# Perceiver layer on one core: ScalarE copies the last pair's transposed weights, and unit 6's projection of values moves behind the last output projection

## The chip, the core and the metric

The kernel runs on one core of one Trainium2 chip. The core has TensorE (PE, matrix products), VectorE (DVE), ScalarE (ACT), GpSimd (POOL) and SyncE (SP, which here issues most transfers). The metric is device time in microseconds (us), lower is better. Times of before and after are medians of several runs. The trace is one execution taken by the hardware profiler.

## What is computed

One layer of a perceiver, in float32, on `x` of 64 sequences x 32 tokens x 256 features, with a context of 257 rows of 192 features for each sequence. The reference, cut down:

```python
x = x + cross_attention(layernorm(x), ctx, mask, Wq, Wk, Wv, Wo)     # 16 heads of 16
x = x + local_attention(layernorm(x), Wq, bq, Wk, bk, Wv, bv)        # one head, each token sees 2 on each side
h = layernorm(x).reshape(2048, 256)
e = argmax(h @ Wr + br)                                              # one of 8 experts for each token
x = x + (gelu(gelu(h @ W1[e] + b1[e]) @ W2[e] + b2[e]) @ W3[e] + b3[e])
```

## The kernel before, in words

The work has three stages. PE, DVE, ACT and POOL each run their instructions in the order in which the program writes them down (`manual_schedule`, L190), so every order below is one written by hand; SP's queue keeps program order too. An engine that waits holds up all that stands behind it on that engine.

**The loop over pairs** (L941 to L987) does the cross attention of two sequences at a time, 32 pairs, as a pipeline: in step m the scores of pair m (`scores_mm`, `numerators`) are made while pair n = m-1 has its softmax weights turned (`transposed`, L783) and pair n-1 is multiplied with its values (`attend`, L799), reduced to its own heads (`own`, L818) and, every second pair, projected and added to `xs` (`project_out`, L834). `transposed` turns four 128x512 pieces through PE (L791) into PSUM and copies each to the tile `pt` in SBUF, by DVE (L797), or for one piece of some steps by ACT (L795). `attend` reads `pt`. GpSimd scales the weights `p` ahead of the turn (L778). Two more steps than pairs are needed: in step m = 32 the last pair (31) is turned, in step m = 33 it is attended, owned and projected out.

**The local attention** goes by units of 256 tokens, 8 of them, and is woven into the loop by `between` (L879). For a unit: normalise (`normed_in`), turn to `xnT` (`turn_in`), `project_q` into `tT`, `project_v` (L371: four products on PE, two ACT copies to `av`, three small GpSimd steps on its extra columns), `attend_scores` (L399), `attend_least` (DVE), `attend_exps` (ACT), `attend_weights`, `attend_sums`, `attend_3` (DVE), `normed_out` (L475, which writes the unit's rows to the DRAM table `table_x` by a transfer on SP's queue). `route_2` to `route_4` find the expert of each token and put it into a table of slots. Unit 6 is the last that starts in the loop: its `project_v` is in step m = 32 (L891) and its `attend_scores` in step m = 33 behind the last `own` (L958). Its remaining steps and the whole of unit 7 stand behind the loop (L1066 to L1098), since unit 7 needs the last `project_out`. PSUM has eight banks, which `bank` hands out (L193).

**The experts** (from L1361) go by tiles of 128 slots, with weights in a ring of three sets (L991). `fetch` (L1001) loads one set with four transfers on SP's queue: `wa` 1030 KB, `bo` 128 KB, `wb` 2048 KB, `wc` 512 KB. `fetch(2, 0)` and `fetch(1, 1)` (L1018) stand right behind the loop; their memory is that of the loop's pools, so the first of them waits until the loop's last users are done. Then come, on the same queue, the two `table_x` writes of units 7 and 6 (L479), then a third fetch (L1363), which waits for the small tile `go` (L1127), made from the finished table of slots. GpSimd gathers an expert tile's rows from `table_x` (`gather_rows`, L1030) when the writes have landed, and PE turns them (`turn`, L1149). Between the loop and that turn PE also works on an "early" tile whose rows were gathered before the loop ended: `early_first` (L1045), `early_second` (L1061), and then `second` (L1289).

Of the kernel before, what the change touches and what calls it, by code (L numbers as in the profile page):

```python
# [7 lines left out]
F32 = mybir.dt.float32  # L8
I32 = mybir.dt.int32
U8 = mybir.dt.uint8  # L10
AF = mybir.ActivationFunctionType
# [7 lines left out]
P = 128  # L19
# [21 lines left out]
NV = D + 2 * E + 1  # L41
# [74 lines left out]
def perceiver_layer_kernel(  # L116
# [14 lines left out]
    nc = tc.nc  # L131
# [237 lines left out]
        proj[u] = [tT]  # L369

    def project_v(u, norm, col):  # L371
        xt = xnT[u]
        v = lw.tile([P, 2, NV], F32, name="av")
        for i in range(2):
            ps = bank("av", (NV,))
            for k in range(2):
                nc.tensor.matmul(
                    ps, xt[:, k, i * P : (i + 1) * P], lv[:, k, :], start=k == 0, stop=k == 1
                )
            nc.scalar.copy(v[:, i, :], ps)  # L380
        part = v[:, :, D : D + E]
        nc.gpsimd.tensor_tensor(
            part, part, bvw.unsqueeze(1).to_broadcast([P, 2, E]), ALU.add
        )
        part = v[:, :, D + E : D + 2 * E]
        nc.gpsimd.tensor_tensor(
            part, part, norm.std[:, col : col + 2].unsqueeze(2).to_broadcast([P, 2, E]), ALU.mult
        )
        nc.gpsimd.tensor_scalar(
            v[:, :, NV - 1], v[:, :, NV - 1], sim_one, None, ALU.add  # L390
        )
        proj[u].append(v)

    def attend_1(u):
        attend_scores(u)
        attend_least(u)
        attend_exps(u)

    def attend_scores(u):  # L399
        tT, v = proj[u]  # L400
        xt = xnT.pop(u)
        ps = bank("as", (2, P))
        for i in range(2):
            cols = slice(i * P, (i + 1) * P)
            for k in range(2):
                nc.tensor.matmul(
                    ps[:, i, :], tT[:, k, cols], xt[:, k, cols], start=k == 0, stop=k == 1
                )
        soft[u] = ps

    def attend_least(u):
        ps = soft[u]
        _, v = proj[u]
        nmx = sp.tile([P, 2], F32, name="anmx")
        p = lw.tile([P, 2, P], F32, name="ap")
        for i in range(2):
            nc.vector.scalar_tensor_tensor(
                p[:, i, :], ps[:, i, :], v[:, i, NV - 1 : NV], k_["band"], ALU.add, ALU.add
            )
        nc.vector.tensor_reduce(nmx, p, AX.X, ALU.min)  # L420
        soft[u] = (p, nmx)
# [171 lines left out]
    NP = B // 2  # L593
    with tc.tile_pool(name="xq", bufs=1) as qpool, tc.tile_pool(
# [185 lines left out]
                    )  # L780
            prob[n] = p

        def transposed(n, parts, by_act=False):  # L783

            if n not in pT:
                pT[n] = wp.tile([P, 2, 2, 512], F32, name="pt")
            for k in parts:
                j, t = divmod(k, 2)
                ps = bank("t")
                for i in range(4):  # L790
                    nc.tensor.transpose(  # L791
                        ps[:, i * P : (i + 1) * P], prob[n][:, j, i, t * P : (t + 1) * P], ident
                    )
                if by_act and k == 3:
                    nc.scalar.copy(pT[n][:, j, t, :], ps)  # L795
                else:
                    nc.vector.tensor_copy(pT[n][:, j, t, :], ps)  # L797
# [81 lines left out]
        def between(m, entered, weights):  # L879


            k, r = divmod(m, 4)
            if r == 0:
                if k >= 1:
                    norms[k] = Norm()
                if k <= 5:
                    norms[k].moments(0, xs[:, 2 * (k + 2), :])
                if 1 <= k <= NU:
                    norms[k].moments(2, xs[:, 2 * (k - 1), :])
                if 0 <= k - 2 <= NU - 2:  # L890
                    project_v(k - 2, norms[k - 1], 2)  # L891
                    if k - 2 < NU - 2:
                        attend_1(k - 2)
                    else:

                        nc.scalar.activation(sp.tile([P, 1], F32, name="spare"), eps_col, AF.Sqrt)
            if r == 1:
                if k <= 5:
                    norms[k].moments(1, xs[:, 2 * (k + 2) + 1, :])
                if 1 <= k <= NU:  # L900
                    norms[k].moments(3, xs[:, 2 * (k - 1) + 1, :])
                if 1 <= k + 1 <= NU - 1:
                    queries_in(k + 1, norms[k - 1], 0, xn=entered)
                if weights:
                    attend_3(k - 2, norms[k], 4, attend_sums(weights))
                if k <= 7:
                    norms[k].newton(slice(0 if k <= 5 else 2, 2 if k == 0 else 4 if k == 1 else 6))
                if 0 <= k - 3 <= NU - 3:
                    enter_table(route_4(2 * (k - 3), 2))
                if k == EARLY + 2:  # L910
                    nc.vector.tensor_copy(token0, table[:, 0:1])
                    early_gather()
            if r == 2:
                if 0 <= k - 1 <= NU - 2:
                    turn_in(k - 1, entered)
                if 1 <= k + 1 <= NU - 1:
                    queries(k + 1)
                if 0 <= k - 2 <= NU - 3:
                    route_2([k - 2], [norms[k].rstd[:, 4:6]])
            if r == 3:  # L920
                if k == EARLY + 1:
                    ps = bank("gap", (1,))
                    nc.tensor.matmul(
                        ps, k_["ones"], before[:, 2 * EARLY, 0:1], start=True, stop=True
                    )
                    gap = sp.tile([P, 1], F32, name="gap")
                    nc.vector.tensor_scalar(gap, ps, -1.0 / P, 1.0, ALU.mult, ALU.add)
                    nc.vector.scalar_tensor_tensor(
                        before[:, 2 * EARLY, 0:1], gap, 0.0, before[:, 2 * EARLY, 0:1],
                        ALU.max, ALU.add,  # L930
                    )
                if k == 0:
                    fold_scores()
                if k == 0:
                    fold_router()
                if 0 <= k - 1 <= NU - 2:
                    project_q(k - 1)
                if 0 <= k - 2 <= NU - 3:
                    route_3(2 * (k - 2), 2)

        for n in range(-1, NP + 1):  # L941
            m = n + 1
            k, r = divmod(m, 4)
            entered = weights = None
            if m < NP:
                if m % 2 == 0 and m // 2 + 2 < B // BG:
                    load(m // 2 + 2)
                if m % 2 == 1 and m // 2 + 1 < B // BG:
                    masks(m // 2 + 1)
                if m + 2 < NP:  # L950
                    centre(m + 2)
                scores_mm(m)
                numerators(m, range(0, 4))
            if 0 <= n - 1:
                attend(n - 1)
                own(n - 1)
            if n - 1 == NP - 1:
                attend_scores(NU - 2)  # L958
            if m < NP:
                numerators(m, (4,))  # L960
            if m + 1 < NP:
                keys_mm(m + 1)
            if r == 1 and 1 <= k + 1 <= NU - 1:
                entered = normed_in(k + 1, norms[k - 1], 0)
            if r == 2 and 0 <= k - 1 <= NU - 2:
                entered = normed_in(k - 1, norms[k], 2)
            if m < NP:
                numerators(m, range(5, 8))
                tail = last_1(m)
            if m + 1 < NP:  # L970
                values_mm(m + 1)
            if r == 3 and 0 <= k - 2 <= NU - 3:
                normed_out(k - 2, norms[k], 4)
            if 0 <= n < NP:
                transposed(n, (0,))
            if m < NP:
                last_2(m, tail)
            if r == 1 and 0 <= k - 2 <= NU - 3:
                weights = attend_weights(k - 2)
            if 0 <= n < NP:  # L980

                transposed(n, (1, 2, 3), r in (1, 2) and 4 < m < NP)
            if n - 1 == NP - 1:
                early_turn()
            if 0 <= n - 1:
                project_out(n - 1)
            between(m, entered, weights)  # L987


# [75 lines left out]

    u, v = NU - 2, NU - 1  # L1066
    norm = norms[NU]
    norm.root(slice(2, 4))
    xn = normed_in(v, norm, 2, True)
    attend_least(u)  # L1070
    turn_in(v, xn, True)
    attend_exps(u)
    project_q(v)
    project_v(v, norm, 2)
    attend_scores(v)
    weights = attend_weights(u)
# [404 lines left out]
```

## Time and profile before

| what | value |
|---|---|
| median of 3 runs | 673.88 us (671.67 to 674.72) |
| the profiled execution: its time | 671.86 us |
| the profiled execution: its span, first to last instruction | 670.1 us |
| mean granted TensorE clock in it | 0.988 of full |
| PE busy | 643.2 us, 96% of the span |
| ACT, POOL, DVE busy | 341.8, 345.0, 320.3 us |
| transfers | 85.51 MB |

The last `own` ends 400.21 us into the span, the rows of the first regular expert tile are turned from 433.57 us on, and the last instruction stands at 670.1 us. A row of the timeline gives the start, the length, the engine, the line, the operation with what it writes and reads, and in brackets how long the engine stood idle before it and for whom. A row of the windows gives for a stretch of time the busy time of each engine, the clock that was granted to TensorE, the share of the 16 DMA engines' time that packets took, and GB/s. A row of the waits gives who waited for whom, in total, how often, and the longest.

### The profile page before, as it was taken

How to read it: one execution, taken by the hardware profiler on the slowest of the kernel's cores; microseconds unless marked ns; L12 is line 12 of the kernel's file. 1: busy time of each engine (PE TensorE's matmuls, PEld its weight loads, DVE VectorE, ACT ScalarE, POOL GpSimd, SP SyncE). 2: the span in 40 equal slices, each digit the busy share in tenths (PEclk: the TensorE clock that was granted, in tenths of full speed). 3: DMA queues.
4: the chain of work that ended last, by engine and by line, in shares of the span. 5: the costliest groups of instructions: out<-in, count | busy, mean ns of one | idle time of the engine just before them, and what ended most of it. 6: DMA issues, size and time to landing. Idle time of an engine off the chain costs nothing. (4 is left out here: it accounts for less than half of the span.)

```text
span 670.1 us, 18642 instructions
## 1 busy us (share of the span) xinstructions
PE 643.2 (96%) x7033; PEld 532.3 (79%) x7033; DVE 320.3 (48%) x1211; ACT 341.8 (51%) x1054; POOL 345.0 (51%) x724
## 2 busy tenths in 40 slices
PE   6999999999999999999999997899999999999994
PEld 4777777677777777877877876899989898899894
DVE  3595676776876877777786785600000000000000
ACT  2864785585684775775766644433322222243220
POOL 2694585688588588588587561331313222231120
PEclk9998999999999999999999998899999999999998
DMA  8923213203313312222200019765793628961001
GB/s 320 295 98 103 76 35 100 104 10 128 105 25 114 104 53 89 101 73 72 97 34 1 19 37 351 253 222 177 245 344 96 217 86 255 336 221 40 27 17 27
DMA packets 37350, 85.51 MB, mean 128 GB/s; under 512 B 2513, under 2 KB 7890, under 8 KB 37024
## 3 DMA queue, kind: packets, MB, share of 16 engines
q1 hardware_dynamic: 34240, 74.64, 33.1%
q0 software_dynamic: 2912, 8.65, 4.0%
q8 instruction: 72, 1.18, 0.7%
q14 instruction: 126, 1.03, 0.5%
HBM read 103.64 MB, written 6.56 MB: 164 GB/s over the span
## 5 line engine op out<-in xcount | busy, mean ns | idle before, releaser
L752 ACT ACTIVATE p<-p,nmx 128x256 f32<-128x256 f32 x256 | 127.2, 500 | 69.0 <-DVE nmx L747 68.0
L778 POOL TENSOR_SCALAR p<-p,rd 128x256 f32<-128x256 f32 x256 | 117.8, 482 | 81.5 <-DVE rd L775 31.4
L1289 PE MATMUL moe<-h,wb 128*128 128x128 f32 (+3 forms) x992 | 128.9, 288 | 0.3 <-issue 0.3
L1289 PEld LDWEIGHTS moe<-h,wb 128*128 128x128 f32 x992 | 124.1, 191 | 2.1 <-issue 0.5
L1313 DVE TENSOR_TENSOR y<-moe,xb 128x256 f32<-128x256 f32 (+2 forms) x20 | 8.5, 423 | 218.5 <-PE moe L1309 208.0
L747 DVE CUSTOM_DVE_ANT_0 p<-s,mb 128x256 f32<-128x256 f32 x256 | 108.0, 478 | 4.6 <-PE s L725 4.6
L797 DVE COPY pt<-t 128x512 f32<-128x512 f32 x114 | 72.6, 674 | 49.8 <-PE t L791 49.8
L692 PE MATMUL k<-cp,pack 64*128 64x512 f32 x384 | 93.8, 609 | 0.0
L709 PEld LDWEIGHTS v<-pack,cp 64*128 64x128 f32 x768 | 78.2, 187 | 19.4 <-issue 8.5
L678 POOL TENSOR_SCALAR cp<-ct,pack 128x256 f32<-128x256 f32 x189 | 88.4, 485 | 8.6 <-DMA ct<-in_ctxt 6.8
L709 PE MATMUL v<-pack,cp 64*128 64x256 f32 x768 | 90.6, 376 | 0.0
L1314 POOL DMA_INDIRECT out_x<-y,token x20 | 20.2, 1009 | 131.3 <-DVE y L1313 110.9
L1279 ACT ACTIVATE h<-moe,wa 128x128 f32<-128x128 f32 (+3 forms) x120 | 38.6, 380 | 69.2 <-PE moe L1273 62.4
L1300 ACT ACTIVATE h<-moe,wa 128x128 f32<-128x128 f32 (+3 forms) x64 | 23.2, 381 | 96.4 <-PE moe L1289 90.7
L1273 PEld LDWEIGHTS moe<-xT,wa 128*128 128x128 f32 x480 | 60.4, 191 | 8.7 <-issue 5.1
L1273 PE MATMUL moe<-xT,wa 128*128 128x128 f32 (+3 forms) x480 | 64.2, 291 | 3.1 <-ACT h L1279 2.4
L791 PE MATMUL t<-pack,p 128*128 128x128 f32 x512 | 64.6, 277 | 0.2
L791 PEld LDWEIGHTS t<-pack,p 128*128 128x128 f32 x512 | 55.6, 141 | 11.0 <-issue 5.0
L692 PEld LDWEIGHTS k<-cp,pack 64*128 64x128 f32 x384 | 38.7, 188 | 32.0 <-issue 25.5
L752 ACT ACTIVATION_READ_ACCUMULATOR p<-p,nmx 128x1 f32 x256 | 48.5, 190 | 0.0
L1030 POOL DMA_INDIRECT xt<-table_x,token x24 | 25.1, 1046 | 43.7 <-issue 18.9
L810 PEld LDWEIGHTS pv<-pt,v 128*32 128x32 f32 x2048 | 30.9, 111 | 13.5 <-issue 5.0
(200 smaller groups left out, 833.9 us busy)
## 6 DMA issues: line engine op xcount, KB each, us to landing
wb<-in_WB SPq DMA_DIRECT2D x17, 2048.0 KB
ct<-in_ctxt SPq DMA_DIRECT2D x15, 1542.0 KB
wa<-in_WA SPq DMA_DIRECT2D x17, 1030.0 KB
wc<-in_WC SPq DMA_DIRECT2D x17, 512.0 KB
table_x<-aw SPq DMA_DIRECT2D x8, 512.0 KB
bo<-in_b SPq DMA_DIRECT2D x17, 128.0 KB
m<-in_mask SPq DMA_DIRECT2D x16, 128.5 KB
xs<-in_x SPq DMA_DIRECT2D x1, 1536.0 KB
```

The lines of the kernel that those rows point to most:

```text
L678: engine.tensor_scalar(cp[:, r, j, :], loaded[b // BG][0][:, r, b % BG, 0:KL], -1.0, clast[:, r, b : b + 1], ALU.mult, ALU.add,)
L692: nc.tensor.matmul(ps[c], wk[h, r, :], cp[h, r, :, :].rearrange("p b k -> p (b k)"), start=r == 0, stop=r == 2,)
L709: nc.tensor.matmul(ps[t][:, j * D : (j + 1) * D], cp[h, r, j, t * P : (t + 1) * P], wv[h, r, :], start=r == 0, stop=r == 2,)
L747: nc.vector.tensor_tensor_reduce(out=p[:, j, i, :], in0=ps[i][:, j * KL : (j + 1) * KL], in1=mb[:, b % BG, 0:KL], scale=1.0, scalar=mb[:, ...
L752: nc.scalar.activation(p[:, j, i, :], p[:, j, i, :], AF.Exp, bias=nmx[:, j, i : i + 1], scale=-1.0, accum_out=sums[:, j, i : i + 1],)
L778: nc.gpsimd.tensor_scalar(p[:, j, i, :], p[:, j, i, :], rd[:, j, i : i + 1], 1.0, ALU.mult, ALU.mult)
L791: nc.tensor.transpose(ps[:, i * P : (i + 1) * P], prob[n][:, j, i, t * P : (t + 1) * P], ident)
L797: nc.vector.tensor_copy(pT[n][:, j, t, :], ps)
L810: nc.tensor.matmul(pv[32 * i : 32 * i + 32, c, j, :], v[:, t, j, at : at + 32], pt[:, j, t, i * P + 64 * c : i * P + 64 * c + 64], start=t ...
L1273: nc.tensor.matmul(ps[:, i, 0:n], wa[:, at : at + P], x_j[:, c, 0:n], start=c == 0, stop=c == 1,)
L1279: nc.scalar.activation(h1[:, f + i, 0:n], ps[:, i, 0:n], AF.Gelu, bias=wa[:, at : at + 1])
L1289: nc.tensor.matmul(pss[f], wb[:, c, f * P : (f + 1) * P], h1[:, c, 0:n], start=c == 0, stop=c == F1 // P - 1,)
```

## The change

It has three parts, all within the last two steps of the loop and the first lines behind it.

1. In step m = 32 the four pieces of pair 31's turned weights are copied by ACT instead of DVE.
2. Unit 6's `project_v` leaves step m = 32. Its four products go behind the loop, that is behind the last `project_out` and `route_4`'s two products on PE. Its ACT copies and GpSimd steps go behind `turn_in` of unit 7. Its `attend_scores` moves forward to where `project_v` was, ahead of pair 31's `attend`. `project_v` is split into a PE part and the rest; for the other units the order of instructions stays the same.
3. Behind the loop, `attend_least` and `attend_exps` of unit 6 go behind unit 7's `project_q`; one activation on a spare tile ahead of `project_q` makes ACT load the table for exponentials there.

```diff
     def project_v(u, norm, col):
+        project_v_out(u, norm, col, project_v_mm(u))
+
+    def project_v_mm(u):
         xt = xnT[u]
-        v = lw.tile([P, 2, NV], F32, name="av")
-        for i in range(2):
-            ps = bank("av", (NV,))
+        pss = [bank("av", (NV,)) for _ in range(2)]
+        for i, ps in enumerate(pss):
             for k in range(2):
                 nc.tensor.matmul(
                     ps, xt[:, k, i * P : (i + 1) * P], lv[:, k, :], start=k == 0, stop=k == 1
                 )
+        return pss
+
+    def project_v_out(u, norm, col, pss):
+        v = lw.tile([P, 2, NV], F32, name="av")
+        for i, ps in enumerate(pss):
             nc.scalar.copy(v[:, i, :], ps)
...
-                if by_act and k == 3:
+                if k in by_act:
                     nc.scalar.copy(pT[n][:, j, t, :], ps)
...
                 if 0 <= k - 2 <= NU - 2:
-                    project_v(k - 2, norms[k - 1], 2)
                     if k - 2 < NU - 2:
+                        project_v(k - 2, norms[k - 1], 2)
                         attend_1(k - 2)
                     else:
+                        attend_scores(k - 2)
 
                         nc.scalar.activation(sp.tile([P, 1], F32, name="spare"), eps_col, AF.Sqrt)
...
-            if n - 1 == NP - 1:
-                attend_scores(NU - 2)
...
-                transposed(n, (0,))
+                transposed(n, (0,), (0,) if m == NP else ())
...
-                transposed(n, (1, 2, 3), r in (1, 2) and 4 < m < NP)
+
+                transposed(
+                    n, (1, 2, 3),
+                    (1, 2, 3) if m == NP else (3,) if r in (1, 2) and 4 < m < NP else (),
+                )
...
     u, v = NU - 2, NU - 1
     norm = norms[NU]
+    values = project_v_mm(u)
     norm.root(slice(2, 4))
     xn = normed_in(v, norm, 2, True)
+    turn_in(v, xn, True)
+    project_v_out(u, norms[NU - 1], 2, values)
+
+    nc.scalar.activation(sp.tile([P, 1], F32, name="spare"), eps_col, AF.Exp)
+    project_q(v)
     attend_least(u)
-    turn_in(v, xn, True)
     attend_exps(u)
-    project_q(v)
     project_v(v, norm, 2)
     attend_scores(v)
     weights = attend_weights(u)
```

More of the change, by code (lines that the diff above doesn't have):

```diff
@@ L399, in attend_scores @@
     def attend_scores(u):
-        tT, v = proj[u]
-        xt = xnT.pop(u)
+        tT = proj[u][0]
+        xt = xnT[u]
         ps = bank("as", (2, P))
@@ L413, in attend_least @@
         _, v = proj[u]
+        del xnT[u]
         nmx = sp.tile([P, 2], F32, name="anmx")
@@ L781, in last_2, with transposed @@
             prob[n] = p
-        def transposed(n, parts, by_act=False):
+        def transposed(n, parts, by_act=()):
             if n not in pT:
```

## Prediction

> **What bounds the kernel now.** I read the page first: PE is busy 96% of the span, so at most places only PE's own work counts, and the question is where PE waits. All edits lie between 394 and 425 us. I then followed the chain of waits back from the end: from 433.57 on it is PE, one piece behind another. Ahead of that it is this (start, length, what):
>
> ```profile
> 420.60 0.34 DVE aw L252
> ...
> 421.47 6.34 DMA table_x<-aw
> ...
> 428.61 4.92 DMA xt<-table_x,token
> 433.57 0.44 PE moe L1149 x2
> ```
>
> So PE's turn at 433.57 waits for a gather, the gather for two writes to `table_x`, and these seem to wait for DVE's end of the local attention. But the write takes 6.34 us. One such write in the loop (L479 at 392.44) is through the DMA engines by about 394.8, that is in 2.4. Why is this one longer? I looked at the windows, 2 us each:
>
> ```profile
> core 0: us, PE busy (x) PEld busy (x) DVE busy (x) ACT busy (x) POOL busy (x), PEclk, DMA share, GB/s
> 400.00:402.00 2.00, 2.00 (x16) 1.90 (x16) 0.57 (x2) 0.71 (x3) 0.00 (x0) 1.00 0.17 27
> 402.00:404.00 2.00, 0.42 (x4) 0.23 (x3) 1.66 (x7) 0.42 (x2) 0.00 (x0) 1.00 0.92 306
> 406.00:408.00 2.00, 2.00 (x6) 1.55 (x6) 0.19 (x1) 1.97 (x5) 0.00 (x0) 0.50 0.92 298
> 416.00:418.00 2.00, 2.00 (x19) 1.97 (x18) 1.89 (x6) 0.21 (x1) 0.00 (x0) 1.00 1.05 382
> 424.00:426.00 2.00, 2.00 (x13) 2.00 (x12) 0.98 (x5) 0.19 (x1) 0.67 (x1) 0.58 0.88 339
> 426.00:428.00 2.00, 2.00 (x21) 2.00 (x20) 0.66 (x4) 0.00 (x0) 0.00 (x0) 1.00 0.06 23
> ```
>
> From 402 to nearly 426 all 16 DMA engines are full, with the two weight fetches (7.4 MB). The `table_x` writes stand behind them on SP's queue. They land at 427.81, when the last engine has drained (0.06 of 16 engines is one). Even if DVE had been done 4 us sooner, they would have landed no sooner. What started the stream? SP's waits and its timeline:
>
> ```profile
> SPq L1008 <- DVE own L824: 7.3, 1, 7.3
> ```
>
> ```profile
> 400.28 0.56 SPq L1008 DMA_DIRECT2D wa<-in_WA  x1
> ...
> 420.99 0.90 SPq L479 DMA_DIRECT2D table_x<-aw  x2
> 428.91 0.61 SPq L1008 DMA_DIRECT2D wa<-in_WA  x1
> ```
>
> The first transfer of the stream waits for `own` of the last pair (399.87 to 400.21). So the chain that counts is: last `own`, 25.5 us of full DMA engines to 427.81, gather, PE. The local attention of units 6 and 7 beside it has some 4.4 us to spare (421.4 against 425.8). Last I read PE's timeline at the edits:
>
> ```profile
> 394.15 2.42 PE L791 MATMUL t<-pack,p 128*128 128x128 f32 x16
> 396.40 2.01 PE L377 MATMUL av<-pack,xnT 128*128 128x273 f32 x8
> 398.34 0.77 PE L810 MATMUL pv<-pt,v 128*32 128x64 f32 x40
> 399.26 0.54 PE L810 MATMUL pv<-pt,v 128*32 128x64 f32 x24
> 399.73 1.16 PE L406 MATMUL as<-xnT,tT 128*128 128x128 f32 x8
> ...
> 404.53 0.66 PE L325 MATMUL xt<-pack,xn 128*128 128x128 f32 x4 [2.11 <-ACT xn L246]
> 405.70 3.41 PE L360 MATMUL am<-xnT,sim 128*128 128x256 f32 x8 [0.52 <-DVE xnT L329]
> ```
>
> **Part 1, the copies.** DVE is busy with routing and `own` of pair 30 until 396.70, so its four copies run from 396.73 to 399.20, though the first pieces lie in PSUM some 1.5 us earlier. ACT has nothing from 392.78 to 397.53. Its copy of the same shape (L795) takes 0.59. The turns are paced by GpSimd, whose last scaling ends at 395.74, and end at 396.57; ACT's fourth copy then ends near 396.57+0.05+0.59 = 397.2, 2.0 us before DVE's. On ACT the table load for square roots behind it (1.28) moves from 398.86 to 397.2 and stays ahead of the root it serves. DVE gets 2.5 us free and uses none of it on this path.
>
> **Part 2, the order on PE.** Before, from the end of the turns to the end of `attend` PE spent 398.34-396.40 = 1.94 on `av`, then 399.80-398.34 = 1.46 on `pv` with a stall on DVE's copy inside: 3.40. After, it has the scores (1.00, the distance of 399.73 to the next start) and `pv` without a stall (1.10, as the same 64 at 385.14): 2.10. The copies at 397.2 are ahead of `pv` at 397.4, so both parts are needed: with DVE's copies `pv` would end at about 399.8 again. Saving: 3.40-2.10 = **1.30**. `own` follows PE at 0.07, so it ends at 398.9 and the stream starts at 399.0 instead of 400.28. The last `project_out` is early by at least as much, and unit 7's normalised rows reach PE at 403.1 instead of 404.5. The four `av` products (2.0) now fill 400.9 to 402.9, where PE would be idle; they fit with 0.2 to spare, so I cost them at nothing; without that cover they would delay unit 7 by 2.0, still inside the spare 4.4.
>
> **Part 3, the tail.** `av`'s two copies (0.39 each) and the exponential table load (1.28, plus 0.2 for the spare) now stand on ACT ahead of unit 7's second `tT`. ACT is through at about 406.9, `am` ends at 406.3, so `tT` is 0.6 late; as PE does unit 7's `av` (2.0) first, the scores are not held. The Trainium skill speaks against a switch of tables in such a place: "ScalarE: Activation LUTs", What ACT_TABLE_LOAD costs, counts a drain on top of the load, about 2.66 us in all. The row of this trace (406.07, 1.28) has the next activation start 0.01 after it. By the row `tT` costs nothing, by the rule it would be 2.0 late and the scores about 0.5; both stay inside the spare. GpSimd's three `av` steps go behind the bias addition (1.26), and unit 6's least and exponentials behind `project_q`: about 0.3 on unit 7's chain.
>
> There is a gain here that I do not count. PE's gap of 2.11 and 0.52 before `am` is followed by a half clock (0.50 in 406 to 408, 0.51 over 405.1 to 408.5), and `am` takes 3.41 where the same took 1.89 at 389.90. The skill's rule ("TensorE: Matmul & The Clock Gate", HAM oscillation — how this bites in real kernels) allows gaps of up to about 3.4 us; here shorter ones were enough, because PE was busy only 1.29 of the 3.4 us from 401.7. By the rule filling the gap gives nothing, by the row 1.5 us. With it the table writes are issued about 1.3+1.5-0.3 = 2.5 sooner, at 418.5. I follow the row, yet the sum gets none of it: the stream drains at 426.5, not sooner.
>
> **Sum.** -1.30 at the stream's start, 0 for the rest: the profiled execution, 671.86 (span 670.1 and 1.76 around it), would become 670.56. It lies 2.02 under the median; I take the step off the median: 673.88-1.30 = **672.6**.
>
> **What is late next.** The table of slots and `go` come 2.5 sooner (427.67 becomes 425.1), and the third fetch follows `go` by 1.24: issued at 426.4 instead of 428.91. The gather is issued at 428.61-1.30 = 427.3. Before, the gather was ahead by 0.3; now it is behind by 0.9 and shares the DMA engines with the fetch. This cost is not in the trace in this order. Bounds: gathers took 3.3 (least), 4.9 (median and this one) and 9.0 (most); one beside the third fetch (434.64) took 6.3. So from -1.6 to +4.1; I take 0, since this gather too ran mostly beside that fetch's packets.
>
> **Rivals.**
> - The gather meets the third fetch's small packets and takes 6.3: +1.4-1.3, 674.0, no change. For it: the row at 434.64. Against it: the fetch's first transfer is `wa`, in whose company 4.9 was seen.
> - Slower: the gather stands behind the third fetch. Place: the DMA engines, 427 to 436. Price 9.0-4.9 = 4.1, less 1.3: 676.7. It decides against the change from a landing of 6.2 us on. Against it: 9.0 was seen only once or so, and the median is 4.9.
> - The bound is DVE's chain after all, as the chain of waits draws it: then 2.5 come off, 671.4, and with one half-clock window fewer on PE in the expert stage (3.41 at half speed, 1.7) 669.7. Against it: the full windows.
> - It doesn't do what it says: ACT's copies come late or the stream waits for another user of the memory, 673.9.
>
> **Chances.** Forecast 0.45, no gain by the gather 0.25, slower 0.12, DVE's chain 0.12, no effect 0.06. A half-clock window more or less, 1.7 either way, lies on any of them, since PE's idle time before 433.57 changes: it was some 1.2 and may become 2 to 3 us, the length that halved the clock above. Range 670.6 to 675.8, which leaves out most of the slower case and the ends of the DVE one. A measurement of this kernel tells about 0.5% (3.4 us) from no change, so: faster (under 670.5) 0.12, from the DVE case with the clock; slower (over 677.3) 0.06; same 0.82. The forecast by itself is a gain of 0.2%.
>
> **What would show it.** Right: `own` of the last pair ends near 399, SP's first `wa` at 399.0, DMA full until 424.5 and the writes landed at 426.5, the gather landed near 432.3, PE's turn at once behind it; `am` in 1.9 at full clock. Wrong: `wa` still at 400.3; a gather of over 6 us; a granted clock of 0.5 behind the turn; a `table_x` write of 2 us or so, which would make DVE the bound.

## The result and the profile after

The changed kernel takes 676.88 us (median of 12 runs, 674.96 to 678.41). The kernel before, run beside it on the same chip, takes 671.87 (12 runs, 670.62 to 674.72), 2.0 less than the median shown further up. The ratio is 1.0059, with a 95% interval of 1.0037 to 1.0081: some 4 us slower by the ratio, while the two medians lie 5.0 apart. 672.6 was predicted, a gain of 1.3.

The profiled execution of after took 677.21 (span 675.3, clock 0.984) against 671.86. To compare traces I count from the start of the last pair's turns on PE (t0), which lies ahead of all edits: 394.15 before, 395.50 after. These 1.35 us are not the change's: between 62 and 66 us the loop lost a second half-clock window, with the same instructions, as a variant of before did too (e6 below). Before, then after:

```profile
62.00:66.00 4.00, 4.00 (x86) 2.59 (x76) 3.39 (x15) 2.67 (x10) 0.00 (x0) 0.77 0.00 0
```

```profile
62.00:66.00 4.00, 4.00 (x84) 2.54 (x70) 3.19 (x15) 2.43 (x9) 0.00 (x0) 0.50 0.00 0
```

From t0 the edits did what was wanted. Here is SP's timeline of after (start, length, what):

```profile
400.31 0.56 SPq L1019 DMA_DIRECT2D wa<-in_WA  x1
...
419.42 0.90 SPq L487 DMA_DIRECT2D table_x<-aw  x2
...
427.45 0.61 SPq L1019 DMA_DIRECT2D wa<-in_WA  x1
```

The stream starts at t0+4.81 (6.13 before), the `table_x` writes are issued at t0+23.92 (26.84), the third fetch at t0+31.95 (34.76). PE's timeline shows the new order, with `pv` free of its stall, the gap ahead of unit 7 down to 0.26 and `am` at full speed (3.41 before):

```profile
398.73 1.10 PE L818 MATMUL pv<-pt,v 128*32 128x64 f32 x64
...
402.16 2.01 PE L379 MATMUL av<-pack,xnT 128*128 128x273 f32 x8
404.43 0.66 PE L325 MATMUL xt<-pack,xn 128*128 128x128 f32 x4 [0.26 <-ACT xn L246]
405.61 1.99 PE L360 MATMUL am<-xnT,sim 128*128 128x256 f32 x8 [0.52 <-DVE xnT L329]
```

The loss comes behind that. The chain of waits of after answers to the lines from 428.61 on before (gather 4.92, then 0.44, and behind it L1309 in 1.82 and L1273 in 3.57, the L1324 and L1288 of after):

```profile
428.52 7.29 DMA xt<-table_x,token
...
435.86 0.69 PE moe L1164 x2
436.55 0.25 PE moe L1256 x2
436.80 3.59 PE moe L1324 x8
440.39 4.46 PE moe L1288 x32
```

The gather is issued 1.44 sooner (t0+33.02 against 34.46) and takes 2.38 more, so PE's turn comes at t0+40.36 instead of 39.42: +0.94. And PE then works at half clock, as the seventh number of the windows says (PEclk). Before, with the turn at 433.57, then after, with the turn at 435.86:

```profile
434.00:436.00 2.00, 2.00 (x13) 1.79 (x12) 0.26 (x2) 0.37 (x1) 1.35 (x2) 1.00 1.04 175
436.00:438.00 2.00, 2.00 (x20) 2.00 (x19) 0.42 (x1) 0.79 (x3) 1.26 (x2) 1.00 0.97 355
```

```profile
434.00:436.00 2.00, 0.14 (x1) 0.14 (x2) 0.00 (x0) 0.00 (x0) 0.00 (x0) 0.82 1.00 387
436.00:438.00 2.00, 2.00 (x7) 1.78 (x8) 0.18 (x1) 0.37 (x1) 0.71 (x1) 0.50 1.03 393
438.00:440.00 2.00, 2.00 (x6) 1.59 (x5) 0.00 (x0) 0.00 (x0) 1.04 (x2) 0.50 1.05 389
```

From the turn to the next L1304 PE needs 9.21 us against 6.26: +2.95. From there to the end both kernels take the same (a difference of -0.04). 0.94+2.95 = 3.89, about what the ratio says (0.0059 of 672 is 4.0).

### The profile page after: what moved, and what is told of

Same layout as the page of the kernel before. It is cut to its first block, busy times and chain, and to the rows that moved or that the text cites. A ratio compares the mean times of both kernels' runs of the same rounds, so it can differ in the third digit from the quotient of the medians.

```text
span 675.3 us, 18644 instructions
## 1 busy us (share of the span) xinstructions
PE 645.9 (96%) x7033; PEld 534.4 (79%) x7033; DVE 318.1 (47%) x1207; ACT 343.6 (51%) x1059; POOL 345.0 (51%) x724
## 5 line engine op out<-in xcount | busy, mean ns | idle before, releaser
L1304 PE MATMUL moe<-h,wb 128*128 128x128 f32 (+3 forms) x992 | 128.9, 288 | 0.2 <-issue 0.2
L1304 PEld LDWEIGHTS moe<-h,wb 128*128 128x128 f32 x992 | 124.1, 191 | 2.0 <-issue 0.4
L805 DVE COPY pt<-t 128x512 f32<-128x512 f32 x110 | 70.1, 673 | 51.0 <-PE t L799 51.0
L1288 PEld LDWEIGHTS moe<-xT,wa 128*128 128x128 f32 x480 | 61.4, 194 | 9.1 <-issue 6.5
L1288 PE MATMUL moe<-xT,wa 128*128 128x128 f32 (+3 forms) x480 | 64.8, 294 | 3.4 <-issue 2.0
```

Source lines behind the costliest of these rows:

```text
L1288: nc.tensor.matmul(ps[:, i, 0:n], wa[:, at : at + P], x_j[:, c, 0:n], start=c == 0, stop=c == 1,)
L1304: nc.tensor.matmul(pss[f], wb[:, c, f * P : (f + 1) * P], h1[:, c, 0:n], start=c == 0, stop=c == F1 // P - 1,)
```

## The experiments

My theory: the change makes SP issue the third fetch 1.07 ahead of the gather, where before it was 0.30 behind; the gather then waits for the fetch's packets, and the longer idle time of PE brings the half clock. Rivals: the earlier stream or the new order in the tail costs something by itself; or the clock alone is the loss. Each kernel was timed in five rounds against before, with one profile. In all tables times are counted from t0.

**e1 and e4: the third fetch behind the gather's landing.** `go` is made from a gathered row, so SP can't issue the fetch before the row is there. e1 is after with this edit, e4 is before with it:

```diff
-    nc.vector.tensor_scalar(go, table[0:1, 0:1], 0.0, None, ALU.is_ge)
...
-    fetch(0, 2, cond=nc.sync.value_load(go[0:1, 0:1], min_val=0, max_val=1) > 0)
     early_second(0, range(4, F1 // P), f2_ps[0:2])
...
     ex, tableT, pick = rest_1()
+    nc.vector.tensor_scalar(go, xt_of[0][1][0:1, 0, 0:1], 0.0, 1.0, ALU.mult, ALU.add)
+    fetch(0, 2, cond=nc.sync.value_load(go[0:1, 0:1], min_val=0, max_val=1) > 0)
```

> The changed kernel, but the tile that the third weight fetch waits for is made from the first gathered rows, so that the fetch is issued only when the gather has landed. Theory A (the changed kernel is slow because the third fetch now stands ahead of the gather on the DMA engines, and because PE then idles long enough to get half clock): the gather lands within 3.3 to 4.9 us of its issue, PE's turn comes about 1.3 us sooner than before, clock full behind it: 670.5 us where before is 671.9 (669.5 to 671.5). Rival B (the loop itself, or the moved projection, has become slower): stays near 676.9.

> The kernel before with the third fetch put behind the landing of the gather as well. Theory A: the fetch was already behind the gather there by 0.3 us, so there is little to win: 0 to 1 us, 670.9 to 671.9. Rival B: 671.9.

e1: 672.13 (12 runs), 0.9995 [0.9981, 1.001]: the whole loss is gone, though the 670.5 that I expected is not reached. PE's turn comes at t0+36.65, 3.7 sooner than in after, and at full clock, although the edits in the loop and the tail are all there. So these cost nothing by themselves. e4: 673.61 (12 runs), 1.0024 [1.001, 1.0039]: in before the same edit costs 1.6 us, where I had expected a gain of 0 to 1.

Why does e1 not gain the 2.77 by which its turn is ahead of before's? PE's timeline of e1:

```profile
431.30 0.44 PE L1163 MATMUL moe<-pack,xt 128*128 128x128 f32 x2 [2.53 <-DMA xt<-table_x,token]
...
448.72 1.02 PE L1287 MATMUL moe<-xT,wa 128*128 128x128 f32 x7 [1.58 <-DMA wb<-in_WB]
```

The fetch, issued at 433.72 instead of 427.45, is now late itself: 17 us behind its turn PE waits 1.58 for its `wb`. In e4 the same wait is 1.31. With the fetch behind the gather's landing in both (6.00 and 7.22 behind its issue), the change is worth 673.61-672.13 = 1.5 us.

**e2: before, with the third fetch directly behind the `table_x` writes.** The order of transfers alone, with nothing of the change:

```diff
-    nc.vector.tensor_scalar(go, table[0:1, 0:1], 0.0, None, ALU.is_ge)
...
-    fetch(0, 2, cond=nc.sync.value_load(go[0:1, 0:1], min_val=0, max_val=1) > 0)
+    fetch(0, 2)
```

> The kernel before, with one thing altered: the third fetch waits for nothing and stands directly behind the table_x writes on SP's queue. Theory A: the gather meets a full queue and takes 6.5 to 9 us instead of 4.9, PE's turn is 2 to 4 us later, and the idle time costs a half-clock window of 1.7 or two: 675 to 678 us. Rival B: nothing that B names is touched, 671.9.

675.8 (6 runs), 1.0058 [1.0038, 1.0079]. The order of the transfers alone, with nothing of the change, gives as large a loss. Its chain of waits:

```profile
429.15 6.82 DMA xt<-table_x,token
...
436.59 3.50 PE moe L1308 x8
440.09 3.57 PE moe L1272 x32
```

The gather takes 6.82, and one half-clock window makes L1308 3.50 long instead of 1.82.

**e3: the half clock taken away.** After, with 14 products on PE in the time of the wait (their results are not used), which end at 434.17, 1.98 ahead of the turn:

```diff
     second(0, P, (3,))
+    for i in range(WARM):
+        nc.tensor.matmul(
+            f1_ps[2][:, 0:P], ring[2][1][:, i % 8, 0:P], h1[:, i % 8, 0:P], start=True, stop=True
+        )
     turn(1, [0])
```

> The changed kernel with 14 products of 128x128 by 128x128 put on PE into the idle time ahead of the turn (some 3.2 us of the 4.8; their result is not used). Theory A: the gather still takes about 7.3, but the clock behind the turn is full, and the 2.95 us that PE lost there between turn and second come back: about 674.0. If half clock is not part of it: 676.9.

675.63 (12 runs, 671.89 to 678.95), 1.0044 [1.0022, 1.0065]. The gather stays as slow as in after and the half clock is gone (chain of waits):

```profile
428.62 7.49 DMA xt<-table_x,token
...
436.73 1.82 PE moe L1325 x8
```

The next L1304 (L1305 here) starts at t0+46.97 instead of 49.57, 2.6 sooner, but the end, counted from t0, is only 1.6 sooner and the median 1.25, less than I expected, and the two intervals overlap. So the half clock does follow PE's idle time in this place, and filling it takes part of that trace's loss away; how much of the median is the clock's I can't say closer than 1.2 to 2.6, and by the intervals it could be none. The clock alone isn't the loss: without the half clock e3 is still slower than before.

**e5 and e6: the fetch just behind the gather's issue.** The one-element step that makes `go` is moved to GpSimd's queue, between the first gather and the second. No wait is added: the order of the queue holds the fetch back. e5 is after with this, e6 before with it:

```diff
-    nc.vector.tensor_scalar(go, table[0:1, 0:1], 0.0, None, ALU.is_ge)
...
     gather(1, 0)
+    nc.gpsimd.tensor_scalar(go, table[0:1, 0:1], 0.0, None, ALU.is_ge)
     gather(2, 0)
```

> The changed kernel, with the tile that the third fetch waits for made by GpSimd right behind the issue of the first gather, so that the fetch is issued some 1.5 to 2.5 us behind the gather instead of 1.1 us ahead of it, and not as late as in the run that waited for the landing. Theory A: the gather lands in 3.5 to 4.5 us, PE's turn is 2 to 2.8 us sooner than before (taken from the turning of the last pair), and the weights are in time for the first switch: 669.5 to 670.5 us where before is 672, ratio 0.996 to 0.998. If the change has a loss of its own besides the order of the two transfers, it stays at or above before.

> The same move of the third fetch in the kernel before, as a control. Theory A: the gather is 1 us quicker (3.5 to 4 instead of 4.9), PE's turn is then bound by PE's own work (0.9 sooner): 671.0 to 671.5 where before is 672, ratio 0.998 to 1.0.

e5: **670.73** (12 runs, 669.75 to 672.04), 0.9971 [0.9955, 0.9987], the fastest kernel of all. e6: 672.97 (12 runs), 0.9999 [0.9981, 1.0016]. So the move alone gives nothing in before, and the change's edits beside it are worth some 0.28% (the two intervals just overlap). GpSimd's timeline of e5, and its chain of waits:

```profile
428.00 1.13 POOL L1041 DMA_INDIRECT xt<-table_x,token  x1 [5.35 <-DVE mid L1190]
429.16 0.34 POOL L1376 TENSOR_SCALAR go<-table 1x1 int32<-1x1 f32 x1
```

```profile
428.00 3.66 DMA xt<-table_x,token
...
432.28 1.82 PE moe L1323 x8
434.10 3.57 PE moe L1287 x32
```

The fetch is issued at 430.76, 2.76 behind the gather, which lands in 3.66. In e6 the gather takes no part: PE has work of its own until its turn (idle 0), so there a quicker gather buys only 0.84 of the turn. At its next change of weights, at 448.47, PE is idle for 0.94 in e5, where e1 waited 1.58. PE's turn is 2.76 sooner than in before, less this 0.94 that is 1.8; by the ratio e5 gains 1.9.

**e7 and e8: the parts by themselves.** e7 is before with part 1 alone (ACT's copies), e8 is after without part 1:

```diff
-                transposed(n, (0,), (0,) if m == NP else ())
+                transposed(n, (0,), ())
...
-                    (1, 2, 3) if m == NP else (3,) if r in (1, 2) and 4 < m < NP else (),
+                    (3,) if r in (1, 2) and 4 < m < NP else (),
```

> The kernel before with part 1 alone: ACT copies the last pair's four pieces, everything else as before. Theory A: attend loses its stall of 0.36 us, the stream starts 0.36 sooner, the chain that leads to the third fetch moves by as much, so that the order of fetch and gather stays: 671.6 where before is 672, within what can be told from no change.

> The changed kernel without part 1: DVE copies the four pieces again. Theory A: the stream starts as in before (attend waits for DVE's fourth copy), but PE's gap is filled, so the third fetch is issued 1 to 2 us sooner against the gather than before and stands ahead of it: the gather takes over 6 us and the clock is halved behind it, 675 to 677 us, ratio 1.004 to 1.008. If the loss came from ACT's copies: 672.

e7: 671.66 (12 runs, 669.0 to 677.74), 0.9992 [0.9967, 1.0016]: no difference by itself, as expected. Its runs lie wide apart, and its profiled execution (673.82) has the fetch 0.59 behind the gather, a gather of 6.21 all the same, and a half-clock window. So a lead this small does not settle it, even in the right order. e8: 677.95 (10 runs), 1.0075 [1.0052, 1.0099]. DVE's copies stall `pv` again, as the prediction had it; PE's timeline of e8:

```profile
398.74 0.92 PE L818 MATMUL pv<-pt,v 128*32 128x64 f32 x32 [0.28 <-DVE pt L805]
399.94 0.54 PE L818 MATMUL pv<-pt,v 128*32 128x64 f32 x24 [0.28 <-DVE pt L805]
...
437.10 0.69 PE L1164 MATMUL moe<-pack,xt 128*128 128x128 f32 x2 [6.83 <-DMA xt<-table_x,token]
```

The stream starts as late as before (t0+6.11), so the gather starts as late as before (34.37), but the quicker tail issues the fetch 2.59 ahead of it, and PE waits 6.83. So parts 2 and 3 bring the loss, by the quicker tail; the earlier stream needs part 1 with them. Part 1 alone has 0.36 of it (in e7 the stream starts at t0+5.77).

All kernels on one scale, one profiled execution each (us; "lead" is the fetch's issue minus the gather's):

| kernel | lead | gather issued | gather to PE's turn | PE idle ahead of it | turn to next L1304 | ratio |
|---|---|---|---|---|---|---|
| e2 | -6.67 | 34.52 | 6.87 | 2.90 | 7.94 | 1.0058 |
| e8 | -2.59 | 34.37 | 7.88 | 6.83 | 8.13 | 1.0075 |
| e3 | -1.21 | 33.18 | 7.54 | 1.98 | 6.25 | 1.0044 |
| after | -1.07 | 33.02 | 7.34 | 4.77 | 9.21 | 1.0059 |
| before | +0.30 | 34.46 | 4.96 | 1.02 | 6.26 | 1 |
| e7 | +0.59 | 34.01 | 6.25 | 2.02 | 7.89 | 0.9992 |
| e5 | +2.76 | 32.95 | 3.71 | 1.08 | 6.28 | 0.9971 |
| e6 | +2.76 | 34.40 | 4.18 (PE's own work) | 0 | 6.35 | 0.9999 |
| e1 | +6.00 | 33.07 | 3.58 | 2.53 | 6.30 | 0.9995 |
| e4 | +7.22 | 34.35 | 4.13 (PE's own work) | 0 | 6.39 | 1.0024 |

## Why the prediction was wrong

Right, by its own steps:
- Part 1 and 2: `own` and the stream 1.30 sooner; the stream was 1.32. That both parts are needed for it: e7 has 0.36, e8 nothing.
- The stream bounds the landing of the `table_x` writes, not DVE: after issued them 2.92 sooner and e4 1.62 later than before (counted from t0), yet e4's gather was issued within 0.11 of before's and after's moved only by 1.44, about the stream's step. The rival with DVE's chain is out.
- `av` fits into PE's gap, and `am` runs at full clock there; the table load and the changes on ACT and GpSimd in the tail cost the path nothing (the load takes 1.28 from 406.56 on, and ACT's next activation starts at 407.85): after's tail was 2.92 faster (about 2.5 was predicted), and e1 and e5 have all of it and lose nothing.
- The order at the end: fetch ahead by 0.9 was predicted, it was 1.07.

Two of the prediction's own signs of being wrong came too: a gather of over 6 us (7.29) and a granted clock of 0.50 behind the turn. And 672.6 stood on a base that was 2.0 too high (before's median of 12 runs is 671.87), which makes the miss look smaller than it is.

Wrong is one step, "What is late next": "I take 0, since this gather too ran mostly beside that fetch's packets". The price was 2.38. The reading was right, but it didn't bear on the question. What differs is how much of the fetch passes ahead of the gather's first packet. In before these are the DMA queues from 428.6 to 430.9, with 28 packets of the fetch and not one of the gather (its queue is q0):

```profile
q1 hardware_dynamic: 28, 0.06, 23.8%
```

Another 49 of the fetch follow until 431.4, and then the gather's packets begin, 2.8 us after its issue. The same for after from 428.5 to 432.9, with 598 packets of the fetch:

```profile
q1 hardware_dynamic: 598, 1.13, 85.0%
```

And from 433 to 435.8:

```profile
q1 hardware_dynamic: 292, 0.51, 59.4%
q0 software_dynamic: 92, 0.31, 30.3%
```

Here the gather has no packet up to 433.4, 4.9 us after its issue, and from there it is done in 2.4, against 2.1 in before. So of the 2.38 some 2.1 is a later start. In e1, where the gather has the engines for itself, q0 moves from 429.6 on, 1.9 after its issue. In e7 q0 moves 1.9 after the issue as well, ahead of every packet of the fetch, and the gather still lands only after 6.21: from 429 to 434 the fetch's packets come in beside its own.

```profile
q1 hardware_dynamic: 432, 0.89, 46.5%
q0 software_dynamic: 88, 0.30, 30.9%
```

So a gather can be held up ahead of its first packet, as in after, and also behind it, as in e7. The Trainium skill ("DMA: Bandwidth & Descriptors", Queues, rings and completion order) has each engine take turns between its queues packet by packet, by which the gather would be held up by a packet or so of each engine, some 0.1 us here (an estimate: 85% of 16 engines for 4.4 us, over 598 packets); the trace shows 4.9 us without one, 3.0 more than e1. Which part of the way from issue to first packet is held up is not shown by these runs, and I leave it open.

The bounds held the true price: -1.6 to +4.1. The value in between was chosen by the wrong likeness, though the trace of before had a row with the right one, the gather of 6.3 beside a fetch under way, and I gave it to a rival for its small packets instead of taking it as the likeliest.

The second term is the clock. I laid "1.7 either way" on all cases, as if the half clock came by chance. It is tied to the same wait: a gather 2.38 longer leaves PE idle for 4.77, and two windows at half clock follow (+2.95). So one cause has both prices, and they add up on the slow side. Chance has a share where the wait is of middle length: 2.53 in e1 brought no half clock, 2.02 in e7 did (more on it in the last section). (The idle time in before is 1.02 in the trace, not "some 1.2".) The slow rival had the mechanism and its place; its size, 4.1-1.3 = 2.8 by a gather of 9.0, should have been 2.38-1.44+2.95 = 3.9 by a gather of 7.3 with its clock. A chance of 0.12 was too little for a case whose condition, the fetch ahead of the gather, was part of my own forecast.

## What to carry to other kernels

A tail that is made faster also issues its later transfers sooner. For each of them ask what it now stands ahead of: here a prefetch that nobody waits for yet got in front of the small gather that everybody waits for, and the gain of 1.3 became a loss of 4. Where two transfers are issued within a microsecond of each other, their order should be held by a queue, and with a lead (here `go` behind the gather on GpSimd, which gave 2.76 us and 670.73; the 0.59 of e7 was too little), not left to which chain happens to be quicker; and a wait on PE is to be priced with the clock that follows it.

## What the runs showed of the hardware

- Issued 1.07 us behind a fetch, a gather had no packet for 4.9 us and landed in 7.29; with 2.76 us of lead it landed in 3.66. With small leads the runs differ: with +0.30 it landed in 4.92, with +0.59 in 6.21.
- The length of PE's idle time doesn't alone decide on the half clock: 2.53 us (e1) gave none, 2.02 (e7) and 2.90 (e2) one window, 4.77 and 6.83 two. One window costs 1.6 to 1.7 us here; two cost 2.95 in after, and 1.87 in e8, where a part of them lay in the idle time (they began at 434.1, the turn at 437.10).
- It also matters where the idle time falls. Between 40 and 655 us of all ten traces each time at half clock is 3.41 us long or twice that, and within a trace they lie on one grid of 3.41 us. In e1 the idle time is split by the grid: the stretch from 429.78 to 433.19 still has 1.89 us of PE's work, and full clock follows. In e7 it lies in one stretch, from 432.44 to 435.85, with 1.43 us of work, and half clock follows. Every such stretch of the grid with at most 1.56 us of PE's work was followed by half clock. Above that the busy time alone doesn't tell: 1.59 to 1.90 was followed by full clock, but 2.09 to 2.26 near 420 us, and 3.08 near 57 us, by half.
- A fetch can be too late as well as too early: 6 to 7 us later than the gather, it made PE wait 1.3 to 1.6 us at the next change of weights. Between the two lay a room of a few microseconds, in which e5 is.
